# Window attention in a four-layer image model: head pairs walked by parity, with other places for queries, taps and k/v tiles

## The chip, the cores and the metric

The kernel runs on one core of a Trainium2 chip. A core has a matrix engine (TensorE, PE in the profile), a vector engine (VectorE, DVE), an activation engine (ScalarE, ACT), a general engine (GpSimd, POOL) and an engine that mostly issues transfers (SyncE, SP). Each works through its own queue in order and waits for the others by semaphores. The metric is the device time of one execution in microseconds (us), as the median of several runs.

## The reference, cut to what matters

The input is a batch of four images, each 256 channels of 64 x 64 pixels, in f32. Four layers follow one another, each added to its input. The change is in the first two, which have the same form. Each normalises its input by groups, runs a gated recurrence along the image's height (this gives `y`), and then attends within windows:

```python
qkv = xw @ qkv_w.T + qkv_b                # 64 windows of 8 x 8 = 64 tokens, 256 channels
q, k, v = qkv[..., :C], qkv[..., C:2*C], qkv[..., 2*C:]
logit = einsum('bpc,bqc->bpq', q.mean(2) * SCALE, k.mean(2))
_, idx = top_k(logit, 4)                  # each window reads the k and v of 4 windows
...                                       # 8 heads of 32 channels, 256 keys
attn = softmax(einsum('bphqd,bphkd->bphqk', qh * SCALE, kh))
out = einsum('bphqk,bphkd->bphqd', attn, vh)
out = (out + depthwise_conv3x3(v)) @ wo_w.T + wo_b
```

The third and fourth layers are of the Mamba kind (selective scans) and take most of the time; the change leaves them alone.

## The kernel before

The program is unrolled over the four images. `attention_layers` (L79) does both attention layers of an image in a schedule that is written out by hand: the order in which the code issues instructions is the order of each engine's queue, and nothing reorders it.

**Ahead of the window phase.** `scan_phase` (L275) goes through eight strips of eight image rows. Per strip it normalises, convolves (the 1x1 convolutions are matrix products of `conv`, L201, whose rows are L204), scans, and makes keys and values, which `keys_values` (L309) writes to `kv_dram` in device memory. It also computes the queries of strips 0 and 1. `routing` (L395) computes the 64 x 64 logits and the four best windows of each window. The depthwise 3x3 convolution is done by `lepe` (L212) as nine taps for each half of the channels, m = 0 and 1, in the image `vimg`; a tap on VectorE is one instruction (L238 or L240), a tap on POOL two, a multiplication (L225) and an addition (L226).

**The window phase** (`window_phase`, L429) is the stage that the change touches. It handles the 64 windows in 32 pairs, four pairs to a strip of eight windows. For pair i:

- `indices` (L441) loads the four window numbers of each window into SyncE's registers, and `gather` (L453, DMA at L459) fetches each window's k and v with four transfers into a tile `kv`, of which there are six.
- `scores` (L470, rows L483) multiplies queries by keys. The eight heads sit in 32 partitions each; heads of even and odd number (parity h = 0 and 1) have a score tile `sc` of two PSUM banks each, and there is one of each parity. One block of products fills both. As k and q must lie in the same partitions, each query also has a copy in the other half of the partitions, which `double` (L270) makes with four transfers for a strip.
- `smallest` (L490, rows L493) takes the reduction of one parity on VectorE (the query is stored negated), `exps` (L497, rows L504) the four exponentials of one parity with their sums on ScalarE, and `normalise` (L513) a reciprocal on VectorE (L516) and four multiplications on POOL (L519) for one parity.
- `turn` (L525, rows L532) transposes one parity's weights on TensorE into two PSUM tiles `pt_ps`; `turned` copies them out, one on VectorE (L543), one on ScalarE (L545). `values` (L548, rows L558) multiplies the weights of both parities by v, and `own_rows` (L565, row L569) adds the result to `vimg` on VectorE.
- Once a strip is complete, `project` (L573) multiplies it by the output weights and adds it to the residual (`add`, L579, on VectorE). `queries` (L253) makes the queries of a later strip; its `evict` (L261) is two ScalarE instructions, into one of two pairs of buffers `qbuf`.

Iteration i of the pair loop issues, in this order, the gather of pair i+2, the doubling, the indices of pair i+3, the scores of pair i+1, their reduction of parity 0, group-norm steps (`mids`), the turn of pair i's parity 0, the reduction of parity 1, exponentials 0, the copies, `own_rows` of pair i-1, a convolution (queries in the last and first pair of a strip, a projection in the two between), normalise 0, the turn of parity 1, exponentials 1, copies, the residual addition, normalise 1, the query eviction, the values of pair i, one or two of 36 taps of strips 6 and 7 on POOL, and more group-norm steps (`ends`). `plan` (L602) puts into `mids` and `ends` the statistics that the following layer needs: two strips of the second attention layer's group norm in the first layer, seven strips for the third layer in the second.

Of the kernel before, what the change touches and what calls it, by code (L numbers as in the profile page):

```python
# [18 lines left out]
P = 128  # L19
# [25 lines left out]
class Net:  # L45
# [33 lines left out]
    def attention_layers(self, x, w_drams, v_drams):  # L79
        tc, nc = self.tc, self.nc  # L80
        with ExitStack() as ctx:
# [16 lines left out]
            qbuf = [  # L98
                [big.tile([P, 2, NW, 64], F32, name=f"q{i}{m}") for m in range(2)]
                for i in range(2)  # L100
            ]
# [99 lines left out]
            def conv(psum, w, w0, src, m):  # L201
                ps = psum.tile([P, NT], F32, tag="mm", name="conv_ps")
                for k in range(2):
                    nc.tensor.matmul(  # L204
                        ps, w[:, k, w0 + m * P : w0 + (m + 1) * P], src[:, k],
                        start=(k == 0), stop=(k == 1),
                    )
                return ps
# [3 lines left out]
            def lepe(lay, s, psum=None, pool=False):  # L212
                vec, box, steps = lay["vec"], {}, []

                def tap(m, kh, kw):
# [6 lines left out]
                    def apart():  # L222
                        both = norm.tile([P, 2, 8, S], F32, tag="sq", name="tap", bufs=1)
                        box[m] = both[:, m]
                        eng.tensor_scalar(box[m], win, w, self.zero, ALU.mult, ALU.add)  # L225
                        eng.tensor_tensor(lep, lep, box[m], ALU.add)  # L226
# [15 lines left out]
                    return apart if pool and not first else step  # L242

                for m in range(2):
                    for kh in range(3):
                        for kw in range(3):
                            steps.append(tap(m, kh, kw))
# [5 lines left out]
            def queries(lay, s, m, psum):  # L253
                src = y[:, :, strip[s], :].rearrange("p c w h -> p c (w h)")
                ps = conv(psum, lay["wb"], WQ - 4 * C, src, m)
                q = qbuf[s % 2][m]

                def evict():
                    for b in range(2):
                        rows = slice(b * 64, b * 64 + 64)  # L260
                        nc.scalar.activation(  # L261
                            q[rows, b].rearrange("p w (j i) -> p w j i", i=8),
                            ps[rows].rearrange("p (j w i) -> p w j i", j=8, i=8),
                            AF.Identity, bias=lay["neg_bq"][rows, m : m + 1], scale=-SCALE,
                        )

                def double():
                    for b in range(2):
                        here, there = slice(b * 64, b * 64 + 64), slice(64 - b * 64, 128 - b * 64)
                        nc.sync.dma_start(q[there, b], q[here, b])  # L270

                return evict, double


            def scan_phase(lay, work, psum, tail):  # L275
# [78 lines left out]
                doubles = []  # L354
                for s in range(NW):
# [30 lines left out]
                    if s >= 5:  # L386
                        for _, double in doubles:
                            double()
# [1694 lines left out]
```

## Time and profile before

| | us |
|---|---|
| median of 3 runs | 12,012.73 (11,994.23 to 12,017.54) |
| profiled execution, its own time | 11,996.08 |
| its span | 11,993.8 |
| busy: PE | 9,862.3 (82%) |
| busy: PE weight loads | 5,605.7 (47%) |
| busy: DVE | 9,842.8 (82%) |
| busy: ACT | 7,047.9 (59%) |
| busy: POOL | 8,892.2 (74%) |
| `hc` L927 on POOL, Mamba layers | 4,812.2 |
| scan `h` L921 on DVE, Mamba layers (first of its groups) | 2,920.3 |
| multiplications `pr` L519 on POOL, window phases | 1,131.3 |
| exponentials `pr` L504 on ACT, window phases | 959.8 |
| reductions `mn` L493 on DVE, window phases | 609.4 |
| transposes `pt_ps` L532 on PE, window phases | 590.6 |
| scores `sc` L483 on PE, window phases | 401.4 |

A profile is of one execution; its span runs from the first to the last instruction, and some 2 us lie around it. A row of the timeline has the start, the time that the instructions of the row took together, the engine, the line of the kernel, the operation with its output and inputs, the shape, and how many instructions it stands for; in square brackets stand the time that the engine was idle ahead of it and what ended that. A row of the busy time by stage has the stretch, its length, the busy time of PE, its weight loads, DVE, ACT and POOL with their numbers of instructions, then the granted clock of TensorE, the busy share of the DMA engines and GB/s.

### The profile page before, as it was taken

The numbers are of one execution on the slowest core, as the hardware profiler recorded it, in microseconds if no ns is written. First come the engines' busy times: TensorE is split into PE (matmuls) and PEld (weight loads), VectorE is DVE, ScalarE is ACT, GpSimd is POOL, SyncE is SP. The second block draws the span as 40 slices with busy tenths as digits, with TensorE's granted clock in tenths as the row PEclk, the third lists the DMA queues.
The fourth block names the chain that finished last, engine by engine and source line by source line (L and its number), as shares of the span: only waits on it lengthen the run. The fifth ranks groups of instructions, "written<-read, shape, count | busy, mean of one in ns | idle before, by whom it ended". The sixth has DMA issues, their size and how long they took to land. (4 is left out here: it accounts for less than half of the span.)

```text
span 11993.8 us, 192457 instructions
## 1 busy us (share of the span) xinstructions
PE 9862.3 (82%) x70632; PEld 5605.7 (47%) x71104; DVE 9842.8 (82%) x8322; ACT 7047.9 (59%) x13064; POOL 8892.2 (74%) x6082
## 2 busy tenths in 40 slices
PE   8988887777898788777789878877778987887777
PEld 4554554444455455444445545544444554554444
DVE  6677998998666799899866679989986667998998
ACT  4555555776455555477645655547764565555776
POOL 3666886898466688689846668868974666886897
PEclk9998998999999999899999989989999998998999
DMA  3343444554334355445433444445543343554454
GB/s 92 104 124 134 175 173 146 173 180 161 87 104 126 135 173 175 147 168 179 160 87 104 128 135 173 176 145 169 182 160 84 101 127 134 173 174 147 169 174 155
DMA packets 682830, 1742.11 MB, mean 145 GB/s; under 512 B 89216, under 2 KB 195216, under 8 KB 681632
## 3 DMA queue, kind: packets, MB, share of 16 engines
q1 hardware_dynamic: 676768, 1721.39, 43.4%
q8 instruction: 563, 9.22, 0.3%
q10 hardware_dynamic: 5120, 8.39, 0.3%
q14 instruction: 379, 3.10, 0.1%
HBM read 1601.51 MB, written 94.37 MB: 141 GB/s over the span
## 5 line engine op out<-in xcount | busy, mean ns | idle before, releaser
L927 POOL TENSOR_TENSOR hc<-h,cb 128x1024 f32<-128x1024 f32 x2056 | 4812.2, 2352 | 805.6 <-DVE h L921 358.3
L921 DVE TENSOR_TENSOR_SCAN h<-da,m_state,pb 128x1024 f32<-128x1024 f32 x1248 | 2920.3, 2340 | 163.2 <-DVE pb L915 1.5
L873 PE MATMUL y<-ident,hc 128*128 128x128 f32 x16384 | 2353.3, 291 | 449.9 <-POOL hc L927 351.9
L873 PEld LDWEIGHTS y<-ident,hc 128*128 128x128 f32 x16384 | 2052.7, 151 | 1128.6 <-POOL hc L927 574.4
L915 DVE TENSOR_TENSOR pb<-du,pb 128x1024 f32<-128x1024 f32 x1672 | 2024.8, 1211 | 122.3 <-PE pb L845 98.9
L857 ACT ACTIVATE da<-delta,m_v 128x1024 f32<-128x1024 f32 x1672 | 1898.9, 1141 | 135.8 <-DVE h L921 119.7
L845 PE MATMUL pb<-m_parts,pick 128*128 128x512 bf16 x2840 | 973.1, 413 | 824.0 <-DVE h L921 766.5
L519 POOL TENSOR_SCALAR pr<-pr,sm,zero 128x256 f32<-128x256 f32 x2048 | 1131.3, 569 | 412.1 <-DVE sm L516 362.2
L504 ACT ACTIVATE pr<-sc,mn 128x256 f32<-128x256 f32 x2048 | 959.8, 493 | 717.2 <-DVE mn L493 351.1
L845 PEld LDWEIGHTS <-pick 128*128 128x128 bf16 x3312 | 262.9, 101 | 1770.5 <-DVE h L921 972.9
L921 DVE TENSOR_TENSOR_SCAN h<-da,pb 128x1024 f32<-128x1024 f32 x424 | 969.7, 2287 | 54.9 <-DVE pb L915 1.0
L831 POOL TENSOR_TENSOR bb<-du,bb 128x1024 f32<-128x1024 f32 x376 | 889.0, 2364 | 101.5 <-DMA bb<-m_cd 94.1
L493 DVE TENSOR_REDUCE mn<-sc 128x4 f32<-128x1024 f32 x512 | 609.4, 1219 | 352.7 <-PE sc L483 352.6
L921 DVE TENSOR_TENSOR_SCAN h<-dap,m_state,bb 128x1024 f32<-128x1024 f32 x288 | 672.2, 2334 | 69.2 <-ACT dap L857 48.4
L532 PE MATMUL pt_ps<-ident,pr 128*128 128x128 f32 x4096 | 590.6, 286 | 135.1 <-ACT pts L545 100.3
L204 PE MATMUL conv_ps<-att_y,att_wb 128*128 128x512 f32 x1536 | 691.4, 594 | 5.3 <-DVE gn_mean L151 5.3
L532 PEld LDWEIGHTS pt_ps<-ident,pr 128*128 128x128 f32 x4096 | 459.4, 144 | 361.7 <-POOL tap L225 102.8
L857 ACT ACTIVATE dap<-delta,m_v 128x1024 f32<-128x1024 f32 x376 | 419.7, 1116 | 314.1 <-DVE h L921 232.1
L483 PE MATMUL sc<-kv,q 32*64 32x128 f32 x16384 | 401.4, 296 | 155.7 <-DMA kv<-kv_dram 90.8
L558 PE MATMUL ov_ps<-pts,kv 128*32 128x64 f32 x16384 | 427.8, 231 | 122.1 <-DVE pts L543 74.1
L240 DVE SCALAR_TENSOR_TENSOR lp<-vimg,att_v,lp 128x512 f32<-128x512 f32 x616 | 465.5, 756 | 27.9 <-DVE lp L240 0.5
L204 PE MATMUL conv_ps<-att_xn,att_wa 128*128 128x512 f32 x1024 | 462.7, 605 | 14.2 <-POOL att_xn L180 14.2
(289 smaller groups left out, 16960.3 us busy)
## 6 DMA issues: line engine op xcount, KB each, us to landing
cb<-m_cd SPq DMA_DIRECT2D x2048, 512.0 KB, 3.8
kv<-kv_dram SPq DMA_DIRECT2D x1984, 128.0 KB, 2.7
bb<-m_cd SPq DMA_DIRECT2D x376, 512.0 KB, 5.1
kv_dram<-kst SPq DMA_DIRECT2D x128, 256.0 KB, 3.4
kv_dram<-vn SPq DMA_DIRECT2D x128, 256.0 KB, 4.2
q<-q SPq DMA_DIRECT2D x256, 128.0 KB, 3.0
m_pe<-in_pe_dram SPq DMA_DIRECT2D x32, 512.0 KB, 6.2
out_dram<-yo SPq DMA_DIRECT2D x64, 256.0 KB, 2.4
```

Of the source, the lines that this page charges most:

```text
L204: nc.tensor.matmul(ps, w[:, k, w0 + m * P : w0 + (m + 1) * P], src[:, k], start=(k == 0), stop=(k == 1),)
L493: nc.vector.tensor_reduce(mn[h], sc[h].rearrange("p r w m n -> p (w m) r n"), AX.XY, ALU.min)
L504: nc.scalar.activation(t[:, g].rearrange("p j r t -> p r j t"), sc[h][:, :, g // 2, g % 2, :].rearrange("p r (j t) -> p r j t", j=2), AF.E ...
L519: nc.gpsimd.tensor_scalar(t[:, g], t[:, g], s[:, g : g + 1], self.zero, ALU.mult, ALU.add)
L532: nc.tensor.transpose(pt[h][j][:, g, :], t[:, g, j].rearrange("p r t -> p (r t)"), self.ident,)
L831: nc.gpsimd.tensor_tensor(pb[i], slots[i][0]["du"], pb[i], ALU.mult)
L845: nc.tensor.matmul(pb[i][:, ss], self.pick[:, n : n + 1].to_broadcast([P, P]), blk["parts"][:, ss], start=True, stop=True,)
L857: nc.scalar.activation(da[i], blk["delta"], AF.Exp, scale=blk["a"](n))
L873: nc.tensor.matmul(blk["y"][:, ss], t[:, ss], self.ident, is_transpose=True, start=(n == 0 and ss.start % NT == 0), stop=(n == DS - 1 and ...
L915: nc.vector.tensor_tensor(pb[i], blk["du"], pb[i], ALU.mult)
L921: nc.vector.tensor_tensor_scan(h[i][:, ss], da[i][:, ss], pb[i][:, ss], state, ALU.mult, ALU.add)
L927: nc.gpsimd.tensor_tensor(hc[i][:, ss], h[i][:, ss], cb[i][:, ss], ALU.mult)
```

## The change

The pair loop is rearranged around the two parities. `scores(i, h)` computes one parity. Iteration i now issues: scores of parity 1 of pair i, the copies of pair i-1's turned parity 0, the turn of pair i-1's parity 1, the reduction of parity 1, `mids`, exponentials and normalise of pair i's parity 0, one tap step on POOL, the convolution, scores of parity 0 of pair i+1, the copies of parity 1 and the values of pair i-1, the turn of pair i's parity 0, the reduction of pair i+1's parity 0, exponentials 1, `own_rows` of pair i-1, normalise 1, one tap step on POOL and in pairs 2 to 10 one tap on VectorE, the residual addition, the query eviction, the gather of pair i+3, the doubling, the indices of pair i+4, and `ends`. So turns and values come a step later, and after the loop the last pair is finished. Products of one parity alternate over b and r, where both parities had r outside and h, b inside.

There are eight `kv` tiles in place of six, and three gathers ahead of the loop in place of two. Both numbers of `qbuf` go: queries of strips 2 to 7 in half m = 1, and of strips 2 to 5 in half 0, overwrite the strip of `y` that they are computed from; half 0 of strips 6 and 7 goes to `late_q`; the copies in the other half of the partitions go to `swap`. The queries of strips 2 to 4 are computed between routing and the first pair and evicted by VectorE, those of strip 5 after the first pair's scores; only strips 6 and 7 are left in the loop. An eviction is one instruction. Doubling a strip up to 5 takes two transfers, of strips 6 and 7 four.

A POOL tap counts as two steps (multiplication, addition). The 17 steps of strip 5 in half m = 1 go to POOL ahead of the first pair (VectorE did these nine taps in the first pairs); the loop has two steps a pair, 51 in all from strips 6 (its half 1) and 7; strip 6's half 0 takes nine taps on VectorE.

The diff, cut to its core, with twelve leading spaces taken off:

```diff
-qbuf = [
-    [big.tile([P, 2, NW, 64], F32, name=f"q{i}{m}") for m in range(2)]
-    for i in range(2)
-]
+swap = [big.tile([P, 2, NW, 64], F32, name=f"q_swap{i}") for i in range(2)]
+late_q = [big.tile([P, NW, 64], F32, name=f"q_late{i}") for i in range(2)]
...
-def conv(psum, w, w0, src, m):
-    ps = psum.tile([P, NT], F32, tag="mm", name="conv_ps")
+def conv(psum, w, w0, src, m, tag="mm", **kw):
+    ps = psum.tile([P, NT], F32, tag=tag, name="conv_ps", **kw)
...
-        def apart():
+        def weigh():
             both = norm.tile([P, 2, 8, S], F32, tag="sq", name="tap", bufs=1)
             box[m] = both[:, m]
             eng.tensor_scalar(box[m], win, w, self.zero, ALU.mult, ALU.add)
+        def add():
             eng.tensor_tensor(lep, lep, box[m], ALU.add)
         def step():
...
             else:
                 eng.scalar_tensor_tensor(out, win, w, acc, ALU.mult, ALU.add)
-        return apart if pool and not first else step
+        return (weigh, add) if pool and not first else (step,)
...
+                steps.extend(tap(m, kh, kw))
...
-def queries(lay, s, m, psum):
+def own(s, m):
+    if m == 0 and s >= NW - 2:
+        return late_q[s % 2]
+    flat = y[:, m, strip[s], :].rearrange("p r c -> p (r c)")
+    return flat.rearrange("p (w t) -> p w t", t=64)
+def query(lay, s, m, psum, eng=nc.scalar, **kw):
     src = y[:, :, strip[s], :].rearrange("p c w h -> p c (w h)")
-    ps = conv(psum, lay["wb"], WQ - 4 * C, src, m)
-    q = qbuf[s % 2][m]
+    ps = conv(psum, lay["wb"], WQ - 4 * C, src, m, **kw)
     def evict():
-        for b in range(2):
-            rows = slice(b * 64, b * 64 + 64)
-            nc.scalar.activation(
-                q[rows, b].rearrange("p w (j i) -> p w j i", i=8),
-                ps[rows].rearrange("p (j w i) -> p w j i", j=8, i=8),
-                AF.Identity, bias=lay["neg_bq"][rows, m : m + 1], scale=-SCALE,
-            )
-    def double():
-        for b in range(2):
-            here, there = slice(b * 64, b * 64 + 64), slice(64 - b * 64, 128 - b * 64)
-            nc.sync.dma_start(q[there, b], q[here, b])
-    return evict, double
+        q = own(s, m).rearrange("p w (j i) -> p w j i", i=8)
+        pq = ps.rearrange("p (j w i) -> p w j i", j=8, i=8)
+        bias = lay["neg_bq"][:, m : m + 1]
+        if eng is nc.scalar:
+            eng.activation(q, pq, AF.Identity, bias=bias, scale=-SCALE)
+        else:
+            eng.tensor_scalar(q, pq, -SCALE, bias, ALU.mult, ALU.add)
+    return evict
+def double(s):
+    for b in range(2):
+        here, there = slice(b * 64, b * 64 + 64), slice(64 - b * 64, 128 - b * 64)
+        if s < NW - 2:
+            nc.sync.dma_start(
+                swap[s % 2][there].rearrange("p m w t -> p m (w t)"),
+                y[here, :, strip[s], :].rearrange("p m r c -> p m (r c)"),
+            )
+            continue
+        for m in range(2):
+            nc.sync.dma_start(swap[s % 2][there, m], own(s, m)[here])
...
-        if s >= 5:
-            for _, double in doubles:
-                double()
-        doubles = [queries(lay, s - 5, m, psum) for m in range(2)] if s in (5, 6) else []
-        for evict, _ in doubles:
-            evict()
+        if s >= 6:
+            double(s - 6)
+        if s in (5, 6):
+            for evict in [query(lay, s - 5, m, psum) for m in range(2)]:
+                evict()
...
-                kv[i, w] = t = work.tile([P, 2, 2 * C], F32, tag="kv", name="kv", bufs=6)
+                kv[i, w] = t = work.tile([P, 2, 2 * C], F32, tag="kv", name="kv", bufs=8)
...
-    def scores(i):
+    def scores(i, h):
         sj, a = divmod(i, 4)
         if i < n_pair:
-            for h in range(2):
-                sc[h] = psum.tile([P, 2, 2, 2, P], F32, tag="sc", name="sc", bufs=2)
+            sc[h] = psum.tile([P, 2, 2, 2, P], F32, tag="sc", name="sc", bufs=2)
             for w in range(2):
                 for m in range(2):
-                    for r in range(2):
-                        for h in range(2):
+                    for b in range(2):
+                        for r in range(2):
                             r0 = r * 64 + h * 32
                             rows = slice(r0, r0 + 32)
-                            for b in range(2):
-                                k0 = b * P + m * 64
-                                nc.tensor.matmul(
-                                    sc[h][b * 64 : b * 64 + 64, r, w, m, :],
-                                    qbuf[sj % 2][m][rows, b, 2 * a + w],
-                                    kv[i, w][rows, :, k0 : k0 + 64],
-                                    start=True, stop=True,
-                                )
+                            k0 = b * P + m * 64
+                            nc.tensor.matmul(
+                                sc[h][b * 64 : b * 64 + 64, r, w, m, :],
+                                (own(sj, m) if r == b else swap[sj % 2][:, m])[
+                                    rows, 2 * a + w
+                                ],
+                                kv[i, w][rows, :, k0 : k0 + 64],
+                                start=True, stop=True,
+                            )
...
-    gather(0)
-    indices(1)
-    gather(1)
-    indices(2)
-    scores(0)
-    early = lepe(lay, NW - 3)[9:]
-    for t in early[:3]:
-        t()
-    for step in (smallest, exps, normalise):
-        for h in range(2):
-            step(0, h)
-    taps = [t for s in (NW - 2, NW - 1) for t in lepe(lay, s, pool=True)]
-    mids, ends, left = {}, {0: early[3:5], 1: early[5:7], 2: early[7:]}, []
+    for i in range(3):
+        gather(i)
+        indices(i + 1)
+    scores(0, 0)
+    scores(0, 1)
+    early = [query(lay, 5, m, psum, nc.vector, tag="pt", bufs=2) for m in range(2)]
+    smallest(0, 0)
+    smallest(0, 1)
+    taps6, taps7 = (lepe(lay, s, pool=True) for s in (NW - 2, NW - 1))
+    taps = taps6[17:] + taps7[17:] + taps7[:17]
+    dve_taps = lepe(lay, NW - 2)[:9]
+    mids, ends, left = {}, {}, []
...
-    double = None
     for i in range(n_pair):
         sj, a = divmod(i, 4)
         add = evict = None
-        gather(i + 2)
-        if double:
-            double()
-            double = None
-        indices(i + 3)
-        scores(i + 1)
-        smallest(i + 1, 0)
+        if i:
+            scores(i, 1)
+            turned(0, 0)
+            turned(0, 1)
+            turn(i - 1, 1)
+            smallest(i, 1)
         for t in mids.get(i, ()):
             t()
-        turn(i, 0)
-        smallest(i + 1, 1)
-        exps(i + 1, 0, (0, 1))
-        turned(0, 0)
-        turned(0, 1)
-        exps(i + 1, 0, (2, 3))
-        own_rows(i - 1)
-        if a == 3 and sj + 2 < NW:
-            evict, double = queries(lay, sj + 2, 0, psum)
-        elif a == 0 and 1 < sj + 1 < NW:
-            evict, double = queries(lay, sj + 1, 1, psum)
+        exps(i, 0)
+        if i == 0:
+            for f in early:
+                f()
+        normalise(i, 0)
+        for t in taps[2 * i : 2 * i + 1]:
+            t()
+        if a == 3 and sj + 2 in (NW - 2, NW - 1):
+            evict = query(lay, sj + 2, 0, psum)
+        elif a == 0 and sj + 1 in (NW - 2, NW - 1):
+            evict = query(lay, sj + 1, 1, psum)
         elif a in (1, 2) and sj:
             add = project(sj - 1, a - 1, psum)
-        normalise(i + 1, 0)
-        turn(i, 1)
-        exps(i + 1, 1, (0, 1))
-        turned(1, 0)
-        turned(1, 1)
-        exps(i + 1, 1, (2, 3))
+        scores(i + 1, 0)
+        if i:
+            turned(1, 0)
+            turned(1, 1)
+            values(i - 1)
+        turn(i, 0)
+        smallest(i + 1, 0)
+        exps(i, 1)
+        if i:
+            own_rows(i - 1)
+        normalise(i, 1)
+        for t in taps[2 * i + 1 : 2 * i + 2]:
+            t()
+        for t in dve_taps[i - 2 : i - 1] if i > 1 else ():
+            t()
         if add:
             add()
-        normalise(i + 1, 1)
         if evict:
             evict()
-        values(i)
-        for t in taps[4 * i // 3 : 4 * (i + 1) // 3]:
-            t()
+        gather(i + 3)
+        if a == 0 and 1 < sj + 1 < NW - 2:
+            double(sj + 1)
+        elif a == 1 and sj + 1 in (NW - 2, NW - 1):
+            double(sj + 1)
+        indices(i + 4)
         for t in ends.get(i, ()):
             t()
+    turned(0, 0)
+    turned(0, 1)
+    turn(n_pair - 1, 1)
+    turned(1, 0)
+    turned(1, 1)
+    values(n_pair - 1)
...
-        for t in lepe(lay, NW - 3, psum)[:9]:
+        taps = lepe(lay, NW - 3, psum)[:9]
+        for s in range(2, 5):
+            evicts = [query(lay, s, m, psum, nc.vector) for m in range(2)]
+            for t in taps[3 * s - 6 : 3 * s - 3]:
+                t()
+            for evict in evicts:
+                evict()
+        for t in lepe(lay, NW - 3, pool=True)[17:]:
             t()
```

More of the change, by code (lines that the diff above doesn't have):

```diff
@@ L246, in lepe @@
                         for kw in range(3):
-                            steps.append(tap(m, kh, kw))
+                            steps.extend(tap(m, kh, kw))
                 return steps
@@ L353, in scan_phase @@
                 nc.gpsimd.memset(vimg[:, :, 8:9, :], 0.0)
-                doubles = []
                 for s in range(NW):
```

## The prediction

> **What bounds the kernel now.** I read the page first (which groups are large, which engines are full), then the timeline and the list of waits of a stretch of attention pairs, then the busy time by stage. The change touches one stage only: the window phase of the attention layers, run eight times (four images, two layers). From the first smallest-score reduction of pair 0 to the last value row it lasts 260.3, 257.4, 258.1 and 262.4 us in the first layer (mean 259.6) and 258.7, 261.1, 258.6 and 259.2 in the second (259.4), some 2,076 of the span's 11,994 us.
>
> One pair in the timeline:
>
> ```profile
> 280.91 1.26 PE L483 MATMUL sc<-kv,q 32*64 32x128 f32 x64
> 282.11 1.09 PE L532 MATMUL pt_ps<-ident,pr 128*128 128x128 f32 x8
> 282.20 2.36 DVE L493 TENSOR_REDUCE mn<-sc 128x4 f32<-128x1024 f32 x2 [1.06 <-PE sc L483]
> 283.04 1.88 PE L204 MATMUL conv_ps<-vimg,att_wb 128*128 128x512 f32 x4
> 283.52 0.47 ACT L504 ACTIVATE pr<-sc,mn 128x256 f32<-128x256 f32 x1 [1.42 <-POOL pr L519]
> ...
> 284.44 0.60 ACT L545 ACTIVATE pts<-pt_ps 128x512 f32<-128x512 f32 x1
> ...
> 285.07 0.42 DVE L569 TENSOR_TENSOR vimg<-ov_ps,vimg 128x256 f32<-128x256 f32 x1
> ...
> 286.33 2.18 POOL L519 TENSOR_SCALAR pr<-pr,sm,zero 128x256 f32<-128x256 f32 x4 [0.81 <-DVE sm L516]
> ...
> 288.31 1.29 PE L483 MATMUL sc<-kv,q 32*64 32x128 f32 x64
> ```
>
> The ring is scores, reduction, exponentials, scores. Both parities' scores come in one block, which can start only when the last of eight exponentials has read the score banks; ScalarE then stands still for scores and reduction. 1.26 + 1.21 + eight exponentials at 0.45 + two copies between them at 0.48 + handovers = 7.4 us (280.91 to 288.31). Many pairs are longer:
>
> ```profile
> 272.72 0.78 PE L483 MATMUL sc<-kv,q 32*64 32x128 f32 x32
> 273.88 0.94 PE L483 MATMUL sc<-kv,q 32*64 32x128 f32 x32 [0.38 <-DMA kv<-kv_dram]
> ```
>
> The second window's keys come late. SyncE issues a gather every 0.65 us, eight and two index loads are 5.95 us a pair, and landing takes 2.7: 8.7 us after the buffer is freed, where one pair lasts under 8. Over the 248 pairs after the first, the score block lasts 0.44 us more than 1.26 in the mean. So a phase is 31 x 7.39 = 229 + 31 x 0.44 = 13.6 + about 5 of group-norm delays + 11.8 from the last pair's reduction to the end = 259.4.
>
> ```profile
> 262.00:478.00 216.00, 186.07 (x3998) 127.59 (x3996) 136.23 (x211) 145.39 (x517) 187.99 (x286) 0.98 0.51 150
> ```
>
> PE, its loads, DVE, ACT and POOL: PE and POOL are 86% and 87% busy with nobody waiting long for them, so a new order soon makes them the bound.
>
> **Part by part: the new ring.** Scores per parity let ScalarE compute one parity while TensorE scores the other, so the old ring falls away. What is late next comes from the order written on each queue.
>
> *Price of one parity's scores.* No row shows it. Bounds: half of the block, 0.6, and its 32 rows one after the other, 32 x 0.109 = 3.5. In the trace the rows of a block start in two interleaved groups of four array tiles, and each tile starts a row every 0.109 us; one parity has four tiles, each still with eight rows: 7 x 0.109 + 0.02 to the last start, then 0.20 until transposes start (281.909 to 282.108) = 1.0. I take 1.0: two parities cost 2.0 where the joint block costs 1.2.
>
> The Trainium skill (TensorE: Matmul & The Clock Gate, Part 3) speaks against the change here: matmuls on distinct tiles overlap, so the span hardly grows with the number of tiles, and using half of them gives no shorter block. By that rule both blocks cost the full 1.2, 2.4 together, about 9 us a phase beyond my sum.
>
> *Pairs with a convolution* (14 projections, 4 queries: 18 of 32). The reciprocal for parity 1 stands on VectorE behind `own_rows`, which waits for the values, which stand on TensorE behind scores, behind the convolution, behind the transposes, which wait for the multiplies that follow that reciprocal. Ring: values 1.15 (0.81 for 56 of 64 rows in the trace, so 0.93, and 0.22 for the last), own_rows 0.33 (0.41, next one overlapping), reciprocal 0.18, multiplies 2.18, transposes 0.93, convolution 1.72 (four rows at 0.43), scores 1.0 = 7.5, handovers cancelling (+0.1 into POOL, -0.2 because transposes start on the first quarter, +0.1 VectorE behind its reduction).
>
> *Pairs without.* Multiplies 2.18, transposes 1.06, copy 0.60, four exponentials 1.94, reciprocal 0.18 give 6.0; POOL's own work, eight multiplies at 0.54 and two tap steps (0.78 and 1.19), gives 6.3. I take 6.3.
>
> *Gathers.* With eight k/v tiles the gather has from one pair's values to the scores nearly two pairs on, 2 x 7.2 - 2 = 12.4 us against 8.7: the 13.6 us go. SyncE's 5.95 still fit under 6.3; the doubling of strips 2 to 5 is two DMAs instead of four (0.58 each), and lies behind the gather.
>
> *First layer.* 18 x 7.5 + 13 x 6.3 = 216.9. Added: 1.3 for pair 0, whose reciprocal stands behind the two early query evictions; nine VectorE taps beside the multiplies, 0.4 each (two multiplies took 1.86 beside L240 instead of 1.1), 3.6; the first convolution pair of seven strips, where the transposes wait for multiplies behind a tap, 0.4 each, 2.8; the next layer's two group norms on POOL (2.48 + 1.65 + 1.90 each, a third on the path), 4. That is 228.6. The tail grows, as values and turns come a step later: values 1.1, transposes 1.06, copy 0.6, exponentials 1.94, copy 0.6, exponentials 1.94, reciprocal 0.3, multiplies 2.18, transposes 1.06, copy 0.6, values 1.15, handovers 1.3 = 13.9. Phase 242.5, or -17.1.
>
> *Second layer.* Seven group norms: centring 2.48 on POOL ahead of parity 0's multiplies, two reductions (1.19, 1.21) on VectorE ahead of the copy that frees the transposes, and column products that hold TensorE until the projection's 1.39 us addition has freed their bank. Bounds per strip: nothing (before they cost next to nothing) and their sum, 6.3. I take 2.8, since POOL then has 6.3 + 2.5 against a ring of 7.5 and the addition holds about 1. 216.9 + 1.3 + 3.6 + 2.8 + 7 x 2.8 + 13.5 = 257.7, or -1.7.
>
> *Ahead of the phase.* Six query convolutions (1.75 each) and six VectorE evictions (0.68, the row of L543) move between routing and pair 0. TensorE waits there for gathers, 8.24 us before its first score and again until 233.5: 10.5 us of convolutions from 219.9 end at 230.5. VectorE's nine taps and evictions end at 231.8 from 220.7; the reduction came at 233.56. Hidden, by under 2 us; without that cover up to 3 a phase. I take 1.5. The 17 tap steps that go to POOL (16.5 us from 214.6) end before its first multiply at 237. ScalarE loses evictions, off the path.
>
> **Sum.** 4 x (-17.1 - 1.7) + 8 x 1.5 = -63 us. The profiled execution took 11,996.1 us (span 11,993.8); the median shown is 12,012.7, 16.6 higher. On the median: 12,013 - 63 = 11,950.
>
> A second rule against it: TensorEngine Tiling (Array Packing), Key Properties, says that a change of tiling mode drains the array. The score-to-transpose gap is 0.20 and transpose-to-convolution, one mode, 0.11; with five changes a pair for three, the rule adds 2 x 0.09 x 31 = 6 us a phase, of which the 0.20 in my score price holds most.
>
> **Rivals.**
> - *The score blocks are shorter.* If issue and not the tile sets the pace, one parity costs 0.7: about 6.5 us less a phase, -115 in all, 11,898. For it: rows of the joint block start every 16 ns. Against: the 0.109 period. 0.17.
> - *The score blocks are longer, and the kernel slower.* If rows of one matmul hold their tile in order and do not interleave, a block of 1.6 lies twice in every convolution pair's TensorE queue: 16 us more a phase, +130, so +67, 12,080. It decides from 1.4 on. Against: joint rows do interleave. 0.08.
> - *Group norm costs its whole 6.3 a strip in the second layer:* 7 x 3.5 x 4 = +98, so +35, 12,048. For it: three in-order queues now hold the ring. 0.12.
> - *The gathers stay late* (eight tiles do not do what they are for): 13.6 x 8 = +109, so +46, 12,059. For it: single issues of 1.0 to 1.7 us. Against: 3.7 us of slack. 0.05.
> - *Nothing measurable:* a score block of 1.25 to 1.4. 0.13.
>
> **How the numbers follow.** The forecast, with terms off by a third (-110 to -25), has 0.45. A measurement of this kernel can tell about 0.2%, 24 us. Faster: 0.45 + 0.17 = 0.62; same 0.13; slower 0.25. The range goes from 11,865 (short score blocks and no cost ahead of the phase) to 12,060 (group norm or late gathers at full price).
>
> **What would show it.** Right: first-layer phases near 242 us, second-layer near 258; pairs alternating between about 6.3 and 7.5 to 8; one parity's 32 score rows in about 1.05 us; hardly any TensorE wait on k/v; the wait before the parity-1 reciprocal ended by TensorE's values. Wrong: a score block over 1.4, both layers alike, or the reduction of pair 0 later than 16 us after the logits (before 13.7).

## The result, and the profile after

The changed kernel takes 12,003.1 us (median of 20 runs, 11,991.5 to 12,011.7) where the kernel before takes 12,012.1 (median of 20, 11,994.2 to 12,028.5): ratio 0.9991, interval 0.9985 to 0.9998. That is 9 us of the 63 forecast, and within the 0.2% that I had called no change.

The total says little; the phases say more. From the first reduction to the last value row, with the part of it in which TensorE was granted half its clock:

| us a phase, mean of four | first layer | at half clock | second layer | at half clock |
|---|---|---|---|---|
| before | 259.6 | 25.4 | 259.4 | 24.3 |
| after, forecast | 242.5 | | 257.7 | |
| after | 250.6 | 26.5 | 269.5 | 41.6 |

All eight phases together go from 2,075.8 to 2,080.3 us; I had -75. The way from the logits to the first reduction shrinks by 4.9 in all (I had +12), and the way from the first layer's last value row to the second's logits grows from 192.6 to 194.1 an image, 6.0 in all, which I had not foreseen and did not follow up. The two profiled executions so differ by +5.6 in the stages that the change touches, and by +6.6 in the rest of their spans (11,993.8 and 12,006.0). Executions of one kernel spread over 20 to 34 us; the phases of one code agree within a few us (the mean of four first-layer phases of one code was 259.6 in one execution and 261.8 in another). So causes are read from phases, and differences under some 2 us are not told from noise.

The score block is as forecast. Lines from here on are those of the changed kernel: L491 scores, L568 values, L542 transposes, L553 VectorE's copy of them, L589 the residual addition, L134 the column products of the group-norm statistics. One block in a stretch at full clock, its first and last rows and the value rows behind them:

```profile
341.41 0.32 PE L491 MATMUL sc<-kv,att_y 32*64 32x128 f32 x1
...
342.24 0.27 PE L491 MATMUL sc<-kv,att_y 32*64 32x128 f32 x1
342.44 0.77 PE L568 MATMUL ov_ps<-pts,kv 128*32 128x64 f32 x40
```

342.44 - 341.41 = 1.03 us for one parity, where I took 1.0. The rule weighed in the prediction, by which a block hardly grows with the number of its tiles (Trainium skill, TensorE: Matmul & The Clock Gate, Part 3), would have made it 1.2. Measured the same way, from the first row to the start of what follows, the joint block of before takes 1.20: half the tiles and half the rows save 0.17, so the block is shorter than by the rule, though far from halved. The list of TensorE's waits between 262 and 470 us has none on k/v left. Steady pairs with a convolution take 7.6 us (median of the first layer at full clock; forecast 7.5), those without 6.3 in the mean (forecast 6.3). But some pairs without one take far longer. The same block in pair 8:

```profile
293.68 0.45 PE L491 MATMUL sc<-kv,att_y 32*64 32x128 f32 x1
...
295.25 0.41 PE L491 MATMUL sc<-kv,att_y 32*64 32x128 f32 x1
295.59 1.93 PE L568 MATMUL ov_ps<-pts,kv 128*32 128x64 f32 x64
297.46 1.97 PE L542 MATMUL pt_ps<-ident,pr 128*128 128x128 f32 x8
```

Scores take 1.9 us, and the 64 value rows and eight transposes nearly twice what they take elsewhere (1.10 and 1.09). The busy time by stage names the cause. Its columns: stretch, length, busy time of PE, weight loads, DVE, ACT and POOL, the granted clock, DMA share, GB/s. Of the changed kernel:

```profile
223.00:250.00 27.00, 24.97 (x325) 14.66 (x324) 21.22 (x31) 11.32 (x44) 21.70 (x31) 1.00 0.76 209
262.00:470.00 208.00, 193.33 (x3859) 139.54 (x3861) 137.06 (x213) 132.39 (x483) 168.75 (x259) 0.93 0.53 149
279.00:290.00 11.00, 10.49 (x256) 7.48 (x256) 8.64 (x14) 7.04 (x27) 9.58 (x15) 1.00 0.61 175
293.70:303.90 10.20, 10.20 (x147) 8.52 (x147) 5.20 (x9) 5.41 (x20) 7.56 (x12) 0.50 0.59 160
```

and of the kernel before, at the start of a phase:

```profile
223.00:250.00 27.00, 14.35 (x264) 10.80 (x272) 14.83 (x22) 8.61 (x34) 8.38 (x15) 0.51 0.62 164
```

Before, TensorE waited for gathers ahead of the phase and came to its first pairs at half clock. The early queries end most of that: 1.00 in this phase, and over all eight, from 10 us ahead of the first reduction to 17 behind it, 4.6 us at half clock for 21.6. The first pair is also shorter, 5.2 us in the first layer for 8.3, but not by the clock: with the queries back in the loop (an experiment below) and 26 of these 27 us at half clock it takes 5.4, so the new order shortens it. In exchange the clock now falls in the middle of the phase, 10.2 us long here, around pairs that have no convolution any more. PE busy for all 10.20 us of the last row is no saturated engine: the same work lasts nearly twice as long. Over the phase's middle (second row) PE is 93% busy at a clock of 0.93; the row of before that the prediction shows had 86% at 0.98.

The second layer's list of waits (who waited for whom, us in total, times, longest) shows the other half:

```profile
PE gn_pm L134 <- DVE x L589: 5.7, 5, 1.7
PE gn_pv L134 <- DVE x L589: 5.1, 5, 1.0
```

Column products of the statistics wait on TensorE for the residual addition's PSUM bank, as the prediction had said, 10.8 us a phase. What it had not seen is how far such a wait travels.

### The profile page after: what moved, and what is told of

The parts are those of the page before. It is cut to its first block, busy times and chain, and to the rows that moved or that the text cites. A ratio compares the mean times of both kernels' runs of the same rounds, so it can differ in the third digit from the quotient of the medians.

```text
span 12006.0 us, 192840 instructions
## 1 busy us (share of the span) xinstructions
PE 10107.7 (84%) x71104; PEld 5773.4 (48%) x71104; DVE 9878.0 (82%) x8386; ACT 6942.4 (58%) x12872; POOL 8890.2 (74%) x6082
## 5 line engine op out<-in xcount | busy, mean ns | idle before, releaser
L876 PE MATMUL pb<-m_parts,pick 128*128 128x512 bf16 x3312 | 1081.2, 411 | 830.0 <-DVE h L952 771.7
L542 PE MATMUL pt_ps<-ident,pr 128*128 128x128 f32 x4096 | 719.3, 301 | 125.9 <-POOL pr L529 111.2
L555 ACT ACTIVATE pts<-pt_ps 128x512 f32<-128x512 f32 x512 | 306.5, 599 | 772.3 <-PE pt_ps L542 771.2
L542 PEld LDWEIGHTS pt_ps<-ident,pr 128*128 128x128 f32 x4096 | 482.9, 148 | 310.1 <-POOL pr L529 255.8
L491 PE MATMUL sc<-kv,q_swap 32*64 32x128 f32 x8192 | 602.5, 290 | 3.1 <-DMA kv<-kv_dram 2.7
L491 PE MATMUL sc<-kv,att_y 32*64 32x128 f32 x7168 | 568.5, 288 | 6.8 <-DVE att_y L270 2.8
L491 PEld LDWEIGHTS sc<-kv,att_y 32*64 32x64 f32 x7168 | 431.3, 140 | 140.1 <-ACT pr L514 78.0
```

Source lines behind the costliest of these rows:

```text
L491: nc.tensor.matmul(sc[h][b * 64 : b * 64 + 64, r, w, m, :], (own(sj, m) if r == b else swap[sj % 2][:, m])[rows, 2 * a + w], kv[i, w][rows ...
L542: nc.tensor.transpose(pt[h][j][:, g, :], t[:, g, j].rearrange("p r t -> p (r t)"), self.ident,)
L876: nc.tensor.matmul(pb[i][:, ss], self.pick[:, n : n + 1].to_broadcast([P, P]), blk["parts"][:, ss], start=True, stop=True,)
```

## The experiments

Theory "clock": half-clock stretches take what is missing in the phases, and they come because pairs without a convolution load the array too little. Rival "queues": the prices of group norm and of in-order waits were too low, and the clock only follows. Phases are means of four, first / second layer. Kernels without a total here were executed once. The recurrence of the expectations is a small model that adds row times along the queues and knows no clock; its working is not shown here.

**Keeping the clock up.** In the loop, ahead of `scores(i + 1, 0)`:

```diff
                     elif a in (1, 2) and sj:
                         add = project(sj - 1, a - 1, psum)
+                    else:
+                        nc.tensor.matmul(
+                            psum.tile([P, NT], F32, tag="mm", name="fill"),
+                            self.ident, wb[:, 0, 0:NT], start=True, stop=True,
+                        )
```

> The changed kernel with one idle matrix product (identity by 512 columns of the output weights, two rows of 0.43 us, into the convolution bank, read by nobody) in each of the 14 pairs of a phase that have no convolution, ahead of the scores. In the trace of the changed kernel the clock granted to TensorE falls to 0.50 for 27 to 45 us of each phase, always around such pairs. Theory 'clock': the pairs are long because TensorE runs at half speed there, and it does because those pairs give the array too little work. Then the stretches at 0.50 inside the phases go, first-layer phases fall from 250.5 to about 245 us and second-layer phases from 269.5 to about 260 (my recurrence, which has no clock, with the fill: 245.4 and 260.0), some 60 us in all: about 11,945. Rival theory 'queues': the long pairs come from group norm and in-order waits, and the half clock is only their trace. Then the phases stay or grow by the fill, up to 14 x 0.9 = 12 us each: 12,000 to 12,100.

Measured: 248.5 / 264.4, with 3.4 / 5.6 us at half clock; 11,967.2 us, 0.9970 of before (0.9960 to 0.9981). One first-layer phase lasted 252.8 with 10.2 us at half clock; later kernels with the same first layer gave 246.6 to 247.5. The stage in which pair 8 lay, with the fill:

```profile
288.00:303.90 15.90, 14.99 (x332) 10.48 (x324) 9.91 (x16) 11.10 (x43) 15.30 (x24) 1.00 0.54 149
```

Work was added and the kernel became faster: the clock is a cause. The gain is smaller than the 245 and 260 expected, and 16 us a phase stay between the layers, so it is not the only one.

**The statistics left out,** in the changed kernel and in the kernel before (with the steps of the tail that belong to them):

```diff
-                    for s in range(NW - 1):
+                    nc.vector.memset(self.gvar, 1.0)
+                    for s in ():
```

> The changed kernel with the group-norm statistics of seven strips left out of the second layer's window phase (the statistics that the third layer divides by are set to one, so the output is not the reference's). Theory 'clock': group norm itself costs what my recurrence gives, 257.3 - 232.8 = 24.5 us a phase, and the half clock the rest; without the statistics second-layer phases come to about 232.8 plus what half clock still adds, 238 to 246. Theory 'queues': all of the second layer's excess is group norm, so its phases fall by 37 us or more, to 232 or less. First-layer phases stay at 250.5 under both.

> The kernel before with the same statistics left out of the second layer's phase (output not the reference's). If group norm is nearly free in the old order, as I had put it, second-layer phases go from 259.4 to no less than 253 (my recurrence: 6.4 less). If they fall by 15 us or more, it was not free before either, and my term for it in the old order was wrong.

Measured: changed kernel 249.9 / 238.2, so the statistics cost 31.3 us a phase there; kernel before 261.8 / 258.1, so they cost 1.3, which is within the noise. Nearly free in the old order, as I had put it, and 4.5 us a strip in the new one, where I took 2.8.

**The old loop, everything else changed.** `scores` does both parities, and the body of the loop is that of before:

```diff
-                    if i:
-                        scores(i, 1)
...
+                    scores(i + 1)
+                    smallest(i + 1, 0)
```

> The changed kernel with the pair loop of before: both parities' scores in one block, turns and values in the same iteration, the other parts of the change kept (eight k/v tiles, early queries, the places of the taps). Theory 'clock': early queries keep the clock up at the start of a phase, but the pairs without a convolution fall under the gate here too or only just stay above it; k/v waits (13.6 us a phase) go. By my recurrence 246 and 249.5 us a phase without clock dips; with them 250 to 260. If this comes out below the changed kernel (250.5 and 269.5), the walk by parity itself is what loses in the second layer; if first-layer phases are above 252, the walk by parity gains in the first.

Measured: 257.1 / 258.8, 41.0 / 39.2 us at half clock; 11,990.7 us, 0.9988 (0.9979 to 0.9997). With half clock on both sides the walk by parity gains 6.5 in the first layer and loses 10.7 in the second. Early queries and eight tiles bring the old loop little: its time at half clock rose from 25 to 40 us.

**The queries back in the loop:**

```diff
-                    if a == 3 and sj + 2 in (NW - 2, NW - 1):
+                    if a == 3 and sj + 2 < NW:
...
-                    elif a == 0 and sj + 1 in (NW - 2, NW - 1):
+                    elif a == 0 and 1 < sj + 1 < NW:
```

> The changed kernel with the queries of strips 2 to 5 put back into the pair loop (convolutions in pairs 3, 4, 7, 8, 11, 12, 15 and 16, evicted by ScalarE into the late-query tiles and y), nothing computed between routing and the first pair. Theory 'clock': those convolutions keep the clock of TensorE up in pairs 3 to 16, as the fill did; at the start of the phase TensorE is cold again, as in the kernel before. So the stretches at 0.50 move to the first 20 us of the phase, and every one of pairs 3 to 16 takes 7.5 to 8 us: my recurrence without clock gives 251.6 and 264.4 us a phase; with the cold start 255 and 267. Rival: moving the queries was a plain gain of eight convolutions of TensorE time; then the phases grow by 8 x (7.5 - 6.3) = 10 us, to 260 and 279.

Measured: 256.2 / 272.0 (21.0 / 32.1 at half clock), 12,047.8 us, 1.0043 (1.0028 to 1.0059). The first layer is near the clock theory's 255; the second lies between its 267 and the rival's 279. In the first 20 us of a phase 16 to 17 us are at half clock, as expected, but the second layer has another 15 behind them, which the theory had not. Eight convolutions more per phase cost 5.6 and 2.5 us, not 10.

**Centring on VectorE,** `stats(s, lambda: psum, nc.vector)`; **parity 1's reciprocal first:**

```diff
+                    normalise(i, 1)
                     if i:
                         own_rows(i - 1)
-                    normalise(i, 1)
```

> The kernel with the fill, and in the second layer's phase the centring of the group-norm statistics (subtraction of the mean, 2.48 us on POOL) on VectorE instead. The second layer pays about 25 us a phase for statistics once the clock is up (264.4 with the fill, 238 without statistics). If it is the centring, which stands on POOL ahead of the multiplications of parity 0, phases fall from 264.4 to about 257 (my recurrence: 6.8 less). If it is the column products that hold TensorE behind the residual addition, or the reductions on VectorE, they fall by 2 or less, or rise.

> The kernel with the fill, and the reciprocal and multiplications of parity 1 issued ahead of own_rows instead of behind it. The prediction's ring of the convolution pairs (7.5 us) runs through values and own_rows to that reciprocal. If that ring is what holds them, this order takes values and own_rows out of it and phases fall by 3.5 to 5 us (recurrence: 245.4 to 240.4 in the first layer, 260.0 to 256.5 in the second, so 248.5 and 264.4 measured to 244 and 261). If POOL or TensorE's own queue holds them, nothing changes.

Measured: centring 247.5 / 262.5, 1.9 less in the second layer, which is hardly told from noise: not what the statistics cost. It takes 1.94 us on VectorE in the mean, and what stands behind it in that queue waits. The reciprocal ahead of `own_rows` gives 242.5 / 260.8: the ring of the prediction was the right one.

**All of it together:** the fill, that order, centring on VectorE in both layers, and `i = 4 * s + (8 if s < 4 else 10 if s < 5 else 7)` for the statistics.

> All together: the fill, parity 1's reciprocal ahead of own_rows, the centring on VectorE in both layers, and the statistics' column products of the first four strips issued in first and last pairs of a strip (no residual addition holds their bank there). Recurrence 239.2 and 245.6 us a phase; with the 3 to 4 us by which the fill's run lay above its recurrence, 243 and 249.5: 4 x (250.6 - 243) + 4 x (269.5 - 249.5) = 110 us under the changed kernel, about 11,890. If the prices of group norm and of the ring are wrong, it stays near the kernel with the fill alone, 11,967.

Measured: 242.6 / 252.5 (2.6 at half clock in each); 11,902.8 us, 0.9914 (0.9901 to 0.9928). It beats the kernel before and the changed one.

**What the gate counts.** The fill again on a corner of the array, and the full version without it:

```diff
-                            psum.tile([P, NT], F32, tag="mm", name="fill"),
-                            self.ident, wb[:, 0, 0:NT], start=True, stop=True,
+                            psum.tile([P, NT], F32, tag="mm", name="fill")[0:32],
+                            self.ident[0:32, 0:32], wb[0:32, 0, 0:NT], start=True, stop=True,
```

> The kernel with the fill, but the idle product uses a tile of 32 x 32 of the array instead of 128 x 128, with the same 512 columns and so the same time of TensorE (two rows of 0.43 us in each of the 14 pairs without convolution). In the traces the clock falls to 0.50 after stretches of 3.4 us in which the time of the matrix rows, each weighted by the share of the array that it uses, is under about 0.38; scores use an eighth of the array, values a quarter. If that weighting is right, the thin product adds 0.05 us of load where the full one added 0.85: the stretches at 0.50 stay (25 to 42 us a phase) and the phases are those of the changed kernel or a little above, 250 to 254 and 269 to 273. If the gate goes by the time in which TensorE is busy, whatever share of the array, the thin product does what the full one did: under 6 us at 0.50, 248.5 and 264.4.

> The version with everything (reciprocal ahead of own_rows, centring on VectorE, column products moved) without the fill. Theory 'clock': the stretches at 0.50 come back, 20 to 35 us a phase; the fill bought 5 to 8 us of clock for 3 us of TensorE, so phases are 2 to 6 us longer than with it (242.6 and 252.5): 245 and 257, some 30 us in all. If the shorter waits load TensorE enough by themselves, no stretches come back and phases are 3 us shorter, 239.5 and 249.5.

Measured: thin 249.6 / 271.4 (7.7 / 25.7 at half clock), 12,008.0 us, 0.9998 (0.9988 to 1.0008). Neither bound: the thin product took away part of the half clock, and no time. Like the full one it has a price: pair 7 of the first layer, at full clock, takes 6.2 us without a product, 7.1 with the full and 7.2 with the thin one. Without the fill, the full version has 247.9 / 262.6 (19.6 / 44.4), 11,967.7 us, 0.9960 (0.9945 to 0.9974): 5.3 and 10.1 us a phase longer than with it.

**Column products moved alone,** with POOL's centring and the fill; **six tiles:** `name="kv", bufs=6`.

> The kernel with the fill, and in the second layer the column products of four strips' statistics moved from the two middle pairs of a strip, where the residual addition holds their PSUM bank, to its first and last pair; centring stays on POOL. If the products' wait for that bank is what the statistics cost, second-layer phases fall from 264.4 to 259 or less (recurrence: 5.1 less), pairs 14 and 18 from 9.0 to under 8. If the reductions and the centring are, they stay within 2 us of 264.4.

> The changed kernel with six k/v tiles instead of eight. The gather of pair i+2 must then wait for the values of pair i-1, which come behind the scores of pair i+1, and SyncE needs 5.95 us to issue it and 2.7 to land: scores to scores 9.9 us, phases of 300 to 312 us, and nearly every wait ahead of the scores ended by the k/v transfer. If transfers could be issued faster than the trace of before shows, or if TensorE had slack, phases stay under 280.

Measured: moved 246.6 / 259.8, so their place is worth 4.6. Six tiles: 312.6 / 311.2, pairs of 9.7, near the 9.9 worked out. TensorE is at half clock there for 83 and 77 us a phase, so not all of it need be the gathers. In its list of waits the transfer is back:

```profile
PE sc L491 <- DMA kv<-kv_dram: 21.9, 31, 2.1
```

**Splitting the second layer's loss:** no statistics and the fill; then the fill with the two reductions cut to a 64th.

> The kernel with the fill and without the seven strips' statistics in the second layer's phase (left out as in the earlier run). It tells the two parts of the second layer's loss apart: with the clock up, statistics cost what the fill's phases (264.4) stand above this one. By my recurrence 260.0 - 237.6 = 22.4, so phases of 241 to 243, no stretches at 0.50, and the clock's share of the 31.3 us that the statistics cost without fill is 8 to 9. If group norm's waits are all of it, this one comes to 233 or less.

> The kernel with the fill, and the two reductions of each strip's statistics (1.2 us each on VectorE) cut to a 64th of their elements in the second layer; all other steps stay (the statistics are then of a part of the strip). Centring was worth 1.9 us a phase and the place of the column products 4.6 of some 22. If the reductions hold the rest, phases fall from 264.4 by 8 us or more; by my recurrence, in which VectorE has room for them, by 2 to 4.

Measured: 246.8 / 240.6 without statistics, so with the clock up and the fill in place they cost 264.4 - 240.6 = 23.8 us, 3.4 a strip. Short reductions: 247.2 / 261.3, 3.1 less. Centring 1.9, reductions 3.1, the products' place 4.6: no single step holds the 23.8, and taken one by one they do not add up to it.

**The old loop with the fill.**

> The changed kernel with the pair loop of before (as in the earlier run) and the fill in the pairs without a convolution. The old loop with eight k/v tiles and early queries gave 257.1 and 258.8 us a phase, with TensorE at half clock for 40 of them; my recurrence without k/v waits and without clock has 246.1 and 249.5. If the half clock is what took back the gain of the eight tiles, the fill removes it and phases fall to 248 to 252 in both layers: then the walk by parity is worth little in the first layer (246.8 with the fill) and loses 12 in the second (264.4). If the old loop's ring of scores, reduction and exponentials with its waits holds the pairs, phases stay at 255 or above.

Measured: 248.4 / 249.9 (6.8 / 3.4 at half clock), 11,920.3 us, 0.9919 (0.9902 to 0.9935). With the clock kept up, the loop of before is within 1.6 us of the new one in the first layer and 14.5 us faster in the second. So what the change had to give lay in its other parts, eight tiles, early queries and the places of the taps, which no run separates, and the clock hid it; the walk by parity as it stands brings nothing. With its order mended ("All of it together") the walk comes level: the eight phases sum to 1,980 us for the old loop's 1,993, and the intervals of the two ratios overlap. The kernel before with nothing but the fill was not run, nor the old loop with the same mends.

## Why the prediction was wrong

- *The step that failed first is one that the sum does not have: the clock.* The prediction quoted a row with a granted clock of 0.98 and priced every TensorE row at it, so half clock stood in the sum at nothing, while the change took eight convolutions out of the loop. What it cost can be read from the pairs. Each phase has 32 intervals, from one pair's first reduction to the next and from the last to the end. I take the median of each over the phases in which it holds no half clock, in the first layer of the changed kernel and of its run without second-layer statistics. They add up to about 243 us (the forecast: 242.5); some rest on one or two phases. The same sum with the fill is 246.6, so the fill's price is about 4. Measured 250.6: nearly all of the 8.1 us missing in the first layer are the clock's. In the second layer five intervals of the changed kernel never come at full clock. The fill's price there is 2.7 by my recurrence and 5.7 by such sums without statistics (239.6 and 233.9), so 264.4 less the fill is 258.7 to 261.7, an estimate, beside 269.5: 8 to 11. Four images: some 60 to 75 of the 79 us missing in the phases. Without any estimate, the fill won 2.1 and 5.1 us a phase after its own price.
- *Group norm was mis-sized in both layers.* In the second I took 2.8 a strip between 0 and 6.3; with the clock up it was 3.4 beside the fill (23.8 for seven, not 19.6), by the estimate above 3.5 to 4 without it, and 4.5 with the half clock that its waits bring on (31.3). The first layer's two group norms came to 6.2 beside the fill (246.8 - 240.6), some 9 without it (243 - 233.9), for my 4.
- *Part of the sum was right by luck.* Without statistics and without half clock a phase takes 233.9; my other terms add up to 238.1 in the second layer and 238.5 in the first. They were 4 to 5 us too dear, and that cancels the group norm of the first layer. That 12,003 lies inside the range is no credit either: the range is 195 us wide, and its lower end of 11,865 does not follow from the terms named there, which give 12,013 - 115 - 12 = 11,886.
- *The new ring was right.* Block 1.03 for 1.0, steady pairs 7.6 for 7.5 and about 6.3 for 6.3, and the reciprocal's order gave what taking values and `own_rows` out of the ring should give.
- *The old ring was priced at the clock that it had.* I compared the new order with the old at its measured length. What taking away 13.6 us of late gathers would bring the old loop came out only with the clock up: 248.4 for 259.6.
- *Gathers:* right, eight tiles remove the waits, and six cost 62 and 42 us a phase, half clock included.
- *Ahead of the phase:* I had +1.5 a phase for lost cover and missed the sign, -0.6; with the queries back in the loop and half clock there it is -0.15, so most of the gain goes with the early queries.
- *The rivals:* group norm at its full 6.3 a strip did not come, late gathers and long or short score blocks neither. Nothing measurable came, but not through a longer score block, on which I had hung it.

How a wait travels to the clock, in the timeline of the kernel with centring on VectorE, second layer, pairs 10 and 11:

```profile
768.79 1.09 PE L542 MATMUL pt_ps<-ident,pr 128*128 128x128 f32 x8
...
770.09 1.33 DVE L589 SCALAR_TENSOR_TENSOR x<-conv_ps,att_v,x 128x512 f32<-128x512 f32 x1
771.45 1.22 DVE L143 TENSOR_REDUCE gn_s<-x 128x4 f32<-128x1024 f32 x1
771.56 0.36 PE L134 MATMUL gn_pm<-gn_s,one_gn 128*128 128x8 f32 x2 [1.68 <-DVE x L589]
...
772.59 0.68 DVE L553 COPY pts<-pt_ps 128x512 f32<-128x512 f32 x1
773.65 0.69 PE L542 MATMUL pt_ps<-ident,pr 128*128 128x128 f32 x2
```

The column product waits 1.68 us for the residual addition, and scores wait behind it. VectorE then does the next strip's sums before the copy that frees the transposes. At 772.0 the clock drops for 10.2 us; the interval lasts 11.4 us where it takes 7.1 without statistics.

## What to carry to other kernels

Before TensorE work is moved out of a loop, add up what is left in each stretch of some 3.4 us, weighted by how much of the array it uses, as the next section does; where that fell under about 0.36 of the stretch here, half clock followed. Price such a stretch at half clock or leave full-array work in it, which here cost some 4 us a phase. Compare a new order with the old one after both have been freed of a disturbance that the order is not about: here the old loop with the same help was the better one. When an order puts more of a ring through in-order queues, price again the background steps that were free before.

## What the runs showed of the hardware

A window may end at half clock with TensorE most of the time at work. The last stretch of 3.4 us ahead of the drop in pair 8:

```profile
290.30:293.70 3.40, 2.44 (x39) 1.46 (x32) 2.84 (x5) 2.23 (x9) 3.40 (x7) 1.00 0.51 148
```

PE has rows for 2.44 of 3.40 us, and no gap between them over 0.33. What tells such stretches from others is a count of rows by their starts. A row counts 0.109 us for each 128 columns, which is the spacing of transposes in the traces, times the share of the 128 x 128 array that its tile fills: an eighth for scores, a quarter for values. Here 21 score rows and eight transposes start (taken from 0.1 us ahead of the stretch to 0.1 us ahead of its end): (21 / 8 + 8) x 0.109 = 1.16 of 3.41 us, 0.34. A convolution would add 0.5, the fill 0.25.

I took all stretches of 3.41 us at full clock, from 15 us ahead of each phase to 5 us behind it, in the traces of the two kernels and the first twelve experiments: 8,247, of which 411 were followed by a drop. With the best limit for each, PE's busy time sorts 191 of them wrongly, the count without shares 299, and the count with shares 79 to 88, by the weight that the thin product is given; its limit is 0.355, fitted to these same traces. So the share of the array counts. In the thin product's own trace that limit asks for 44 drops if it counts a sixteenth and for 17 if it counts a quarter; 23 came. It did more than a sixteenth should; why is open.

The Trainium skill (TensorE: Matmul & The Clock Gate, "HAM oscillation") gives the abstract rule as no idle gaps over about 3.4 us. Half-clock stretches here do come in multiples of 3.4 us (3.41, 6.83, 10.24); the rule is not enough here, with the clock falling at gaps of 0.33.
